# A two-layer graph-attention and feed-forward kernel: engines in a written order of phases, expert rows in pairs of tiles added to the output by accumulating scatters, and a dense last batch

## Chip, cores and metric

The kernel runs on one core of one Trainium2 chip. The metric is device time in microseconds of one execution; smaller is better. The time of the kernel before is 2003.29 us, the median of three runs (2002.27 to 2005.84).

## What is computed

The input x has 64 batches of 256 nodes with 256 features, all float32. One 256 x 256 adjacency matrix serves all batches. Two layers follow each other, and every step adds to x:

```python
x = x + elu(gat4(layernorm(x), adj))        # layer 0: graph attention, 4 heads of 64
x = x + layernorm(x) @ Wf.T + bf            # layer 0: one linear map
x = x + relu(gat1(layernorm(x), adj))       # layer 1: graph attention, 1 head of 256
x = x + moe(layernorm(x))                   # layer 1: mixture of experts
# moe(t): top 2 of 8 experts by router logits, weights rw normalized to a sum of 1
#   out = t + sum over the two experts e of rw_e * (gelu(t @ w1[e] + b1[e]) @ w2[e] + b2[e])
```

The mixture adds its own input, so the last line leaves x + t + the two weighted expert results for each of the 16384 tokens.

## The kernel before

A batch is 256 tokens, two tiles of 128 (NT = 2). `batch_layers` (L353 to L435) is a Python generator that records one batch: layer norm statistics on VectorE (L273, L274) and GpSimd (L276, L277), transposes on TensorE (L284) that ScalarE copies out of PSUM (L288), projections (L298) whose logits ScalarE exponentiates (L306) and VectorE scales (L310), attention weights z (L325 transposes, L332 on VectorE), their product with the values (L343), the linear map (L386, L392), the second attention, and the last layer norm xng (L416). From it come the router logits (L431, L435), and x + xng, formed by GpSimd (L423), is stored in a scratch array `base` (L424).

Experts are computed on routed rows only. Batches are taken in chunks of four (eight tiles), chunks in three groups of 28, 24 and 12 batches (`GROUPS`). `dispatch` (L447 to L569) runs once per chunk, on VectorE almost alone: top two experts, a count of the rows of each expert, the place of each row in a region of the expert, and a list of slots that are full by now. GpSimd then sends every token's row twice, to the regions of its two experts, by indirect DMAs of 128 rows (`send`, L573). `slot` (L604 to L673) handles one tile of 128 rows of one expert: SyncE loads the expert's weights `we` (L613) and the rows `xr` (L617), with expert and place in registers; TensorE transposes the rows (L631, copied by ScalarE at L633), multiplies by w1 (L644), ScalarE applies gelu (L650), TensorE multiplies by w2 (L656), VectorE adds the bias (L663), and GpSimd scatters the 128 results (L668) to a scratch array `y`, where each token has one row for each of its two experts. When all slots of a group are done, `combine` (L675 to L695) loads for each tile of tokens its two rows of `y` (L681) and its row of `base` (L679), adds them with the routing weights in two VectorE instructions (L692) and stores the result (L695). Partly filled tiles are topped up with filling rows at the end of each group, which makes 277 slots in all (2 x 128 + 3 x 7).

Order of the work: the main loop at the end starts a batch every three steps (`TICKS`), hands out slots and merges at a rate (`Rate`), and calls every active generator once per step. That is only the order in which instructions are recorded; the framework's scheduler then orders each engine's instructions by priority and readiness as its own model sees them. Each engine runs its list strictly in order. PSUM holds eight such buffers of one bank, divided by tag: two for `tr` (all transposes, attention logits, counts), three for `mm` (projections, attention results, linear map, router logits), three for `sl` (expert products). Loads and stores are all issued from SyncE's one queue, indirect DMAs from GpSimd's.

```python
        if step % TICKS == 0 and more:
            nxt = next(batches, None)
...
        for job in slots.start():
            active.append(job())
        for job in merges.start():
            active.append(job())
        for job in list(active):
            if next(job, active) is active:
                active.remove(job)
```

Of the kernel before, what the change touches and what calls it, by code (L numbers as in the profile page):

```python
# [8 lines left out]
F32 = mybir.dt.float32  # L9
# [5 lines left out]
P = 128  # L15
SLOT_ENGINES = [mybir.EngineType.SP, mybir.EngineType.PE, mybir.EngineType.DVE]
AFTER = mybir.DependencyInfo(mybir.DependencyClass.Sync, mybir.DependencyReason.DATA)
# [8 lines left out]
def kernel(  # L26
# [20 lines left out]
    H = 4  # L47
# [9 lines left out]
    GROUPS = ((4,) * 7, (4,) * 6, (4, 4, 2, 2))  # L57
    assert sum(map(sum, GROUPS)) == B
    NTC = max(map(max, GROUPS)) * NT
    SLOTS = 2 * NTC + 2 * (E - 1)  # L60

    ROW = D + 2
    YPAD = 2 * 2 * E * P
# [7 lines left out]
    psum = ctx.enter_context(tc.tile_pool(name="psum", bufs=2, space=bass.MemoryType.PSUM))  # L71

# [27 lines left out]
    for layer, op in enumerate((ALU.is_gt, ALU.not_equal)):  # L100
        mf = work.tile([P, NT, N], F32, tag="xT", name=f"maskf{layer}", bufs=4)
        nc.vector.tensor_scalar(mf, adj_i, 0.0, None, op0=op)
        pm = psum.tile([P, NT, N], F32, tag="tr", name="pm")
        for t in range(NT):
            for j in range(NT):
                nc.tensor.transpose(
                    pm[:, j, t * P : (t + 1) * P], mf[:, t, j * P : (j + 1) * P], ident
                )
        m = const.tile([P, NT, N], F32, tag=f"mask{layer}", name=f"mask{layer}")
        nc.vector.tensor_copy(m, pm)  # L110
        masks.append(m)

    def center(w, cols):


        pc = psum.tile([P, cols], F32, tag="mm", name="pc", bufs=3)
# [47 lines left out]
    pw = psum.tile([P, KT, D], F32, tag="tr", name="pw")  # L164
# [15 lines left out]
    pr = psum.tile([P, KT, E], F32, tag="tr", name="pr")  # L180
# [7 lines left out]
    WBUFS = 6  # L188
# [3 lines left out]
    def pack_expert(e):  # L192
# [8 lines left out]
        )  # L201
        nc.sync.dma_start(
# [3 lines left out]
        nc.sync.dma_start(out=b2s[:, e, :], in_=rows_to_all(b2[e], D))  # L206
        nc.sync.dma_start(out=wpack[e], in_=wt)

    caps = [sum(g) * NT + 1 for g in GROUPS]
    xs_d = [
        tc.dram_tile([(E * cap + E) * P, ROW], F32, name=f"xs_{g}")
        for g, cap in enumerate(caps)
    ]
    y_d = [
        tc.dram_tile([YPAD + 2 * sum(n) * N, D], F32, name=f"y_{g}") for g, n in enumerate(GROUPS)
    ]
    base_d = [tc.dram_tile([sum(n) * N, D], F32, name=f"base_{g}") for g, n in enumerate(GROUPS)]


    fill = const.tile([P, E, ROW], F32, tag="fill", name="fill")
    nc.gpsimd.memset(fill, 0.0)
    nc.vector.memset(fill[:, :, D : D + 1], -1.0)
    nc.gpsimd.iota(
        fill[:, :, D + 1 : D + 2], pattern=[[2 * P, E], [1, 1]], base=0, channel_multiplier=2,
        allow_small_or_imprecise_dtypes=True,
    )

    def fill_spare():  # L230
        for xs, cap in zip(xs_d, caps):
            nc.sync.dma_start(
                out=xs[E * cap * P :, :].rearrange("(t p) c -> p t c", p=P), in_=fill
            )
        nc.vector.tensor_scalar(
            fill[:, :, D + 1 : D + 2], fill[:, :, D + 1 : D + 2], 2.0 * E * P, None, op0=ALU.add
        )

# [9 lines left out]
    )  # L248
    def iota(shape, pattern, base, by_partition, name):
# [6 lines left out]

    em8 = iota([E], [[1, E]], -E, 0, "em8")
    jrow = iota([SLOTS], [[1, SLOTS]], 0, 0, "jrow")
    tok2 = iota([NTC], [[2 * P, NTC]], 0, 2, "tok2")
    part = iota([1], [[1, 1]], 0, 1, "part")  # L260
    region = []
    for g, cap in enumerate(caps):
        region.append(iota([E], [[cap, E]], 0, 0, f"region{g}"))
    scan_mask = const.tile([P, E, NTC], F32, tag="scan_mask", name="scan_mask")
    nc.vector.memset(scan_mask, 1.0)
    nc.vector.memset(scan_mask[:, :, 0:1], 0.0)

# [12 lines left out]
    def transposed(src):  # L280
        pt = psum.tile([P, KT, N], F32, tag="tr", name="pt")
# [9 lines left out]
    def projected(xT, wx, heads, rstd):  # L291
# [3 lines left out]
        for t in range(NT):  # L295
            pq = psum.tile([P, heads, d + 3], F32, tag="mm", name="pq", bufs=3)
# [19 lines left out]
    def attention(q, heads, mask):  # L316

        d = D // heads
        probs = []
        for h0 in range(0, heads, 2):  # L320
            hs = range(h0, min(h0 + 2, heads))
            pd = psum.tile([P, len(hs), N], F32, tag="tr", name="pd")
            for i, h in enumerate(hs):
                for t in range(NT):
                    nc.tensor.transpose(  # L325
                        pd[:, i, t * P : (t + 1) * P],
                        q[:, t, h, d + 1 : d + 2].to_broadcast([P, P]), ident,
                    )
            for i, h in enumerate(hs):
                z = work.tile([P, NT, N], F32, tag="z", name="z", bufs=6)  # L330
                for j in range(NT):
                    nc.vector.scalar_tensor_tensor(  # L332
                        z[:, j, :], pd[:, i, :], q[:, j, h, d + 2 : d + 3], mask[:, j, :],
                        op0=ALU.max, op1=ALU.mult,
                    )
                probs.append(z)
            yield
        pvs = []
        for t in range(NT):
            pv = psum.tile([P, heads, d + 1], F32, tag="mm", name="pv", bufs=3)  # L340
# [12 lines left out]
    def batch_layers(b, g, r0, c0, xng, lg):  # L353
# [6 lines left out]
        yield  # L360
        q = projected(xT, wx0, H, rstd)
        yield
        pvs, rinv = yield from attention(q, H, masks[0])
        hp = work.tile([P, NT, D], F32, tag="hp", name="hp")
        for t, pv in enumerate(pvs):
# [3 lines left out]
            )  # L369
        ex = work.tile([P, NT, D], F32, tag="e", name="e")  # L370
        nc.scalar.activation(ex, hp, AF.Exp)  # L371
        yield
# [4 lines left out]
        _, rstd = norm_stats(x1)  # L377
        yield
        xT = transposed(x1)
        x1b = work.tile([P, NT, D], F32, tag="x1b", name="x1b")  # L380
        nc.gpsimd.tensor_add(x1b, x1, bias_f[:, None, :].to_broadcast([P, NT, D]))
        yield
        pf = psum.tile([P, NT, D], F32, tag="mm", name="pf", bufs=3)
# [12 lines left out]
        yield  # L396
        _, rstd = norm_stats(x2)
        yield
        xT = transposed(x2)
        yield  # L400
        q = projected(xT, wx1, 1, rstd)
        yield
        pvs, rinv = yield from attention(q, 1, masks[1])
# [6 lines left out]
        yield  # L410
        mv, rstd = norm_stats(x2)
        yield
        xe = keep.tile([P, NT, ROW], F32, tag="xng", name="xng", bufs=XNG)
        xn = xe[:, :, :D]
        for t in range(NT):
            nc.vector.tensor_scalar(  # L416
                xn[:, t, :], x2[:, t, :], mv[:, t, 0:1], rstd[:, t : t + 1],
                op0=ALU.subtract, op1=ALU.mult,
            )
        xng.append(xe)  # L420
        yield
        xT = transposed(xn)
        nc.gpsimd.tensor_add(x2, x2, xn)  # L423
        nc.sync.dma_start(  # L424
            out=base_d[g][r0 * P : (r0 + NT) * P, :].rearrange("(t p) d -> p t d", p=P), in_=x2
        )
        yield
        pl = psum.tile([P, NT, E], F32, tag="mm", name="pl", bufs=3)
# [6 lines left out]
        nc.vector.tensor_copy(lg[:, c0 : c0 + NT, :], pl)  # L435

    XNG = max(map(max, GROUPS)) + 3

    def whole(out, in_, name):
# [5 lines left out]
    def dispatch(g, c, nt, done, n, first, last, xng, lg, state):  # L445


        rt = lambda shape, name, bufs=1, dt=F32: keep.tile(
            [P] + shape, dt, tag=name, name=f"{name}_{g}_{c}", bufs=bufs
        )  # L450
        vec, tt = nc.vector, nc.vector.tensor_tensor
        emb = em8[:, None, :].to_broadcast([P, nt, E])
        ohs, tops, lcur = [], [], lg
        for k in range(2):
# [10 lines left out]
            if k == 0:  # L465
                for i, xe in enumerate(xng):
                    vec.tensor_scalar(
                        xe[:, :, D : D + 1], least[:, i * NT : (i + 1) * NT, None], float(E), None,
                        op0=ALU.add,
                    )  # L470
                    vec.tensor_scalar(
                        xe[:, :, D + 1 : D + 2], tok2[:, i * NT : (i + 1) * NT, None],
                        float(YPAD + 2 * P * done), None, op0=ALU.add,
                    )
# [4 lines left out]
            tops.append(top)  # L479
        m = rt([E, nt], "m")  # L480
        tt(m.rearrange("p e t -> p t e"), ohs[0], ohs[1], ALU.add)
        mf = m.rearrange("p e t -> p (e t)")

        pp = psum.tile([P, 2, E, nt], F32, tag="tr", name="pp")
# [5 lines left out]
        yield  # L490
        ed = rt([nt], "ed")
        tt(ed, tops[1], tops[0], ALU.subtract)
        nc.scalar.activation(ed, ed, AF.Exp)
        run = rt([E, nt], "run")
        if nt == NTC:
            vec.tensor_tensor_scan(
                run.rearrange("p e t -> p (e t)"), scan_mask.rearrange("p e t -> p (e t)"),
                both[:, 1].rearrange("p e t -> p (e t)"), 0.0, ALU.mult, ALU.add,
# [8 lines left out]
        rows, used = state  # L507
        at = rt([E], "at")
        vec.scalar_tensor_tensor(at, region[g], float(P), rows, op0=ALU.mult, op1=ALU.add)
        tt(pre, pre, at[:, :, None].to_broadcast([P, E, nt]), ALU.add)  # L510
        tt(rows[:, :, None], rows[:, :, None], run[:, :, nt - 1 : nt], ALU.add)
        wts = rt([2, nt], f"wts_{g}_{c}")
        vec.tensor_scalar(wts[:, 0], ed, 1.0, None, op0=ALU.add)
        vec.reciprocal(wts[:, 0], wts[:, 0])
        tt(wts[:, 1], ed, wts[:, 0], ALU.mult)
# [5 lines left out]
        vec.tensor_copy(pos, posf)  # L521
        if last:
            tt(at, at, run[:, :, nt - 1], ALU.add)
            pads = rt([E], "pads", 1, I32)
            tt(pads, at, part.to_broadcast([P, E]), ALU.add)
        else:
            pads = None
        yield

        full = rt([E], "full")  # L530
        vec.tensor_scalar(
            full, rows, 1.0 / P, (127.0 / P if last else 0.0) - 127.0 / 256.0,
            op0=ALU.mult, op1=ALU.add,
# [306 lines left out]
```

## Time and profile before

| What | Value |
|---|---|
| median of 3 runs | 2003.29 us |
| the profiled execution: its time, its span | 1986.96 us, 1985.2 us |
| mean granted TensorE clock | 0.911 |
| TensorE busy, x10244 | 1609.9 us (81%) |
| VectorE busy, x4618 | 1284.2 us (65%) |
| GpSimd busy, x1278 | 1063.7 us (54%) |
| ScalarE busy, x1770 | 819.5 us (41%) |
| ScalarE activation-table loads (L650 109, L306 102, L493 5, two more) | 218 at 1283 ns |
| DMA queue q1 (SyncE's): bytes, share of 16 engines | 230.32 MB, 38.2% |
| DMA queue q0 (GpSimd's): bytes, share of 16 engines | 73.33 MB, 10.0% |

How to read it: "busy" is the time in which an engine had an instruction in it, over the span, which runs from the first instruction to the last. The granted clock is the share of TensorE's full speed that its throttle let through, so a TensorE that is busy at a granted clock of 0.9 does nine tenths of the work. A matrix product of float32 is recorded as two instructions, a transpose as one. No engine is busy all the time, so the views that matter are those by stretch of time and those of waits.

### The profile page before, as it was taken

How to read it: one execution, taken by the hardware profiler on the slowest of the kernel's cores; microseconds unless marked ns; L12 is line 12 of the kernel's file. 1: busy time of each engine (PE TensorE's matmuls, PEld its weight loads, DVE VectorE, ACT ScalarE, POOL GpSimd, SP SyncE). 2: the span in 40 equal slices, each digit the busy share in tenths (PEclk: the TensorE clock that was granted, in tenths of full speed). 3: DMA queues.
4: the chain of work that ended last, by engine and by line, in shares of the span. 5: the costliest groups of instructions: out<-in, count | busy, mean ns of one | idle time of the engine just before them, and what ended most of it. 6: DMA issues, size and time to landing. Idle time of an engine off the chain costs nothing. (4 is left out here: it accounts for less than half of the span.)

```text
span 1985.2 us, 34359 instructions
## 1 busy us (share of the span) xinstructions
PE 1609.9 (81%) x10244; PEld 1431.6 (72%) x10244; DVE 1284.2 (65%) x4618; ACT 819.5 (41%) x1770; POOL 1063.7 (54%) x1278
## 2 busy tenths in 40 slices
PE   6988979799979897787988979897989879677800
PEld 5877878688868786776877868786878768676700
DVE  7886857476757675664566968786756645552444
ACT  1222344354545455344544535463535434342400
POOL 2455555556465647555555655656575554664400
PEclk9998889898989999898998989998989989898955
DMA  8113223434333434244445566666543434587987
GB/s 270 61 44 108 68 73 116 134 118 141 113 126 124 145 112 143 92 134 127 146 130 174 175 193 207 222 192 191 178 149 112 130 118 137 167 259 244 314 263 235
DMA packets 211096, 306.84 MB, mean 155 GB/s; under 512 B 29880, under 2 KB 140096, under 8 KB 210912
## 3 DMA queue, kind: packets, MB, share of 16 engines
q1 hardware_dynamic: 183184, 230.32, 38.2%
q0 software_dynamic: 26736, 73.33, 10.0%
q8 instruction: 84, 1.38, 0.3%
q10 hardware_dynamic: 992, 0.99, 0.2%
q14 instruction: 100, 0.82, 0.1%
HBM read 192.16 MB, written 112.38 MB: 153 GB/s over the span
## 5 line engine op out<-in xcount | busy, mean ns | idle before, releaser
L343 PE MATMUL pv<-q,z 128*128 128x65 f32 (+1 forms) x2560 | 386.4, 307 | 46.7 <-DVE q L310 33.5
L668 POOL DMA_INDIRECT y<-y,to x277 | 292.4, 1056 | 243.4 <-DVE mv L274 83.3
L343 PEld LDWEIGHTS pv<-q,z 128*128 128x128 f32 x2560 | 347.0, 202 | 69.5 <-DVE q L310 42.5
L644 PE MATMUL ph<-sT,we 128*128 128x128 f32 x2216 | 297.9, 285 | 38.2 <-DVE y L663 18.9
L644 PEld LDWEIGHTS ph<-sT,we 128*128 128x128 f32 x2216 | 288.8, 201 | 49.7 <-DVE y L663 20.0
L573 POOL DMA_INDIRECT xs<-xng,pos x256 | 253.3, 989 | 91.5 <-issue 68.1
L656 PE MATMUL py<-w2s,hT 128*128 x1108 | 298.4, 401 | 2.9 <-ACT hT L650 2.9
L332 DVE SCALAR_TENSOR_TENSOR z<-pd,q,mask 128x256 f32<-128x256 f32 x640 | 268.3, 473 | 33.8 <-PE pd L325 33.4
L298 PE MATMUL pq<-wx,xT 128*128 128x268 f32 (+1 forms) x1024 | 270.6, 399 | 2.3 <-ACT xT L288 2.2
L650 ACT ACTIVATE hT<-ph,we 128x128 f32<-128x128 f32 x554 | 170.0, 365 | 190.9 <-PE ph L644 140.7
L276 POOL TENSOR_SCALAR rstd<-mv 128x2 f32<-128x2 f32 x256 | 64.1, 251 | 297.2 <-DVE mv L274 271.0
L656 PEld LDWEIGHTS py<-w2s,hT 128*128 128x128 f32 x1108 | 204.6, 201 | 24.8 <-ACT hT L650 4.0
L288 ACT COPY xT<-pt 128x512 f32<-128x512 f32 x256 | 146.3, 588 | 148.4 <-PE pt L284 147.7
L298 PEld LDWEIGHTS pq<-wx,xT 128*128 128x128 f32 x1024 | 184.2, 195 | 26.1 <-ACT xT L288 2.7
L273 DVE BATCH_NORM_STATS2 stats<-x 128x6 f32<-128x256 f32 x384 | 148.9, 410 | 81.5 <-POOL x L409 79.7
L636 DVE SCALAR_TENSOR_TENSOR to<-xr,ef 128x1 int32<-128x1 f32 x277 | 76.4, 279 | 187.7 <-DMA xr<-xs 126.8
L277 POOL TENSOR_TENSOR rstd<-rstd,mhalf 128x2 f32<-128x2 f32 x256 | 186.7, 729 | 19.9
L371 ACT ACTIVATE e<-hp 128x512 f32<-128x512 f32 x64 | 40.3, 629 | 336.9 <-DVE hp L366 336.8
L650 ACT ACT_TABLE_LOAD x109 | 139.8, 1283 | 72.3 <-issue 41.7
L692 DVE SCALAR_TENSOR_TENSOR o<-yk,wts,o 128x256 f32<-128x256 f32 x256 | 123.1, 499 | 71.2 <-DMA o<-base 48.4
L310 DVE SCALAR_TENSOR_TENSOR q<-pq,rstd,q 128x256 f32<-128x256 f32 x256 | 116.0, 476 | 59.5 <-ACT q L306 59.1
L306 ACT ACT_TABLE_LOAD x102 | 130.9, 1283 | 49.6 <-PE pq L298 48.7
(135 smaller groups left out, 2338.3 us busy)
## 6 DMA issues: line engine op xcount, KB each, us to landing
we<-wpack SPq DMA_DIRECT2D x277, 288.0 KB
xr<-xs SPq DMA_DIRECT2D x277, 129.0 KB
yk<-y SPq DMA_DIRECT2D x128, 256.0 KB
xin<-in_x_dram SPq DMA_DIRECT2D x64, 256.0 KB
base<-x SPq DMA_DIRECT2D x64, 256.0 KB
o<-base SPq DMA_DIRECT2D x128, 128.0 KB
out_dram<-o SPq DMA_DIRECT2D x128, 128.0 KB
y<-y,to POOLq DMA_INDIRECT x277, 3.5
```

Of the source, the lines that this page charges most:

```text
L273: nc.vector.bn_stats(stats[:, t, :], src[:, t, :])
L277: nc.gpsimd.tensor_tensor(rstd, rstd, mhalf, ALU.pow)
L288: nc.scalar.copy(dst, pt)
L298: nc.tensor.matmul(pq.rearrange("p h c -> p (h c)"), xT[:, k, t * P : (t + 1) * P], wx[:, k, :], start=(k == 0), stop=(k == KT - 1),)
L306: nc.scalar.activation(q[:, t, :, d:], pq[:, :, d:], AF.Exp, scale=rstd[:, t : t + 1])
L332: nc.vector.scalar_tensor_tensor(z[:, j, :], pd[:, i, :], q[:, j, h, d + 2 : d + 3], mask[:, j, :], op0=ALU.max, op1=ALU.mult,)
L343: nc.tensor.matmul(pv[:, h, :], z[:, j, t * P : (t + 1) * P], q[:, j, h, : d + 1], start=(j == 0), stop=(j == NT - 1),)
L573: d = nc.gpsimd.indirect_dma_start(out=xs_d[g][: E * caps[g] * P, :], out_offset=bass.IndirectOffsetOnAxis(ap=at, axis=0), in_=xe, in_offs ...
L644: nc.tensor.matmul(ph[:, f, :], we[:, k * D + f * P : k * D + (f + 1) * P], xT[:, k, :], start=(k == 0), stop=(k == KT - 1),)
L650: nc.scalar.activation(hT[:, f, :], ph[:, f, :], AF.Gelu, bias=we[:, C_B1 + f : C_B1 + f + 1])
L656: mm = nc.tensor.matmul(py, hT[:, f, :], w2s[:, bass.ds(e, 1), f * D : (f + 1) * D].rearrange("p e c -> p (e c)"), start=(f == 0), stop=(f ...
L668: d = nc.gpsimd.indirect_dma_start(out=y_d[g][:, :], out_offset=bass.IndirectOffsetOnAxis(ap=to, axis=0), in_=y, in_offset=None,)
```

## The change

The same results are computed with the following differences (lines are those of the changed kernel):

- **Written order.** The main loop runs inside a manual schedule: each engine executes its instructions in the order in which they are recorded. Each generator yields a rank, and within a step the active generators are called in the order of their ranks. Phases are merged and split a little, and the routing (`route`, formerly `dispatch`) is spread over four steps instead of being recorded in two.
- **PSUM.** All tiles share one pool of eight buffers.
- **Pairs.** An expert's rows are handled in pairs of tiles (256 rows): one load of weights, one of rows, one bias addition of 512 elements, products with 256 moving columns. There is one group over 63 batches with one region for each expert (`CHUNKS` of 4 batches, then 2 and 1), which makes 126 + 7 = 133 pairs. The first chunk has only one pair that is surely full, each later one eight; 14 pairs are left to a flush at the end, where filling rows are written by SyncE.
- **Rows carry more.** Each sent row has its token number, first expert and two weights in four extra columns (260 instead of 258 elements).
- **No `y`, no `base`, no `combine`.** ScalarE forms xng and x + xng by two activations with per-row scale and bias instead of VectorE and GpSimd, and x + xng is stored straight to the output. ScalarE multiplies an expert's results by their weights (L644), and GpSimd adds them to the output's rows by two indirect DMAs per pair that accumulate (L682). A pair's two scatters wait for the two scatters of the pair before it, and for the stores of x + xng recorded since.
- **Dense last batch.** Batch 63 is not routed: after its router, all eight experts are applied to its 256 rows with the weights (zero for six of them) folded in by VectorE (L711), and its result is stored once, after the last scatter.

Instructions of the program, before and after: TensorE's expert products with w1 are 1108 of 128 columns, then 564 of 256; with w2 554, then 564 of 256; table loads 218, then 106; loads of `we` and `xr` 277 each, then 133 each; scatters of results 277, then 266; sends 256 and 24 of filling rows, then 252. The written order has 251 steps: a batch starts at every third step up to 189, the first result of a pair is scattered at step 47, the last layers of batch 63 are at step 206, and 30 of the 133 pairs are scattered after step 208.

The diff, cut to its core:

```diff
-    GROUPS = ((4,) * 7, (4,) * 6, (4, 4, 2, 2))
+    CHUNKS = (4,) * 15 + (2, 1)
...
+    def bank(name, shape):
+        t = psum.tile([P, 2 * D], F32, tag="bank", name=name, bufs=8)
...
-        for t in range(NT):
-            nc.vector.tensor_scalar(
-                xn[:, t, :], x2[:, t, :], mv[:, t, 0:1], rstd[:, t : t + 1],
-                op0=ALU.subtract, op1=ALU.mult,
...
-        nc.gpsimd.tensor_add(x2, x2, xn)
+        for t in range(NT):
+            nc.scalar.activation(
+                xe[:, t, :D], x2[:, t, :], AF.Identity, bias=by[:, 0, t : t + 1],
+                scale=rstd[:, t : t + 1],
+            )
+        for t in range(NT):
+            nc.scalar.activation(
+                base[:, t, :], x2[:, t, :], AF.Identity, bias=by[:, 0, t : t + 1],
+                scale=by[:, 1, t : t + 1],
+            )
...
+    def expert_pair(j, n, ids, ef, regs, needs):
...
+        yield 30
+        hT = hidden(xT, we)
+        yield 80
...
+        y = result(hT, bass.ds(regs["x"][i], 1))
+        yield 2
+        for t in range(2):
+            nc.scalar.activation(y[:, t, :], y[:, t, :], AF.Copy, scale=w[:, t : t + 1])
+        scatters.append((y, to))
...
+    def scatter():
...
+        y, to = scatters.pop(0)
+        ds = []
+        for t in range(2):
+            ds.append(nc.gpsimd.indirect_dma_start(
+                out=out_rows, out_offset=bass.IndirectOffsetOnAxis(ap=to[:, t : t + 1], axis=0),
+                in_=y[:, t, :], in_offset=None, compute_op=ALU.add,
+            ))
...
+            before = added[-2:] + based
...
+            for ins in before:
+                tc.add_manual_dep(ds[-1].ins, ins.name, AFTER, reason="added to before")
...
+    with tc.manual_schedule():
+        while more or active or waiting or scatters:
+            phase = step % TICKS
+            if phase == 0 and more:
...
+            if phase == 2:
+                credit = min(credit + (2.0 if more else 3.0), 3.0)
+                while waiting and credit >= 1.0:
+                    credit -= 1.0
+                    begin(waiting.pop(0)(), 90)
+            if scatters:
...
+                begin(one(), 55 if phase == 1 else 5)
+            for entry in sorted(active, key=lambda a: a[:2]):
+                entry[0] = next(entry[2], None)
```

## The prediction

> **What bounds the kernel now.** I read the page's busy shares first, then the slices, then stretches, and last TensorE's waits. (Columns of a stretch: length, busy time of TensorE, its weight loads, VectorE, ScalarE and GpSimd with counts, granted clock, DMA share, GB/s.)
>
> ```profile
> PE 1609.9 (81%) x10244; PEld 1431.6 (72%) x10244; DVE 1284.2 (65%) x4618; ACT 819.5 (41%) x1770; POOL 1063.7 (54%) x1278
> ...
> PEclk9998889898989999898998989998989989898955
> ```
>
> ```profile
> 700.00:730.00 30.00, 29.52 (x200) 26.33 (x198) 20.79 (x64) 17.60 (x37) 15.59 (x20) 1.00 0.43 132
> 1600.00:1700.00 100.00, 91.05 (x612) 82.28 (x611) 56.10 (x218) 48.05 (x110) 46.79 (x54) 0.99 0.41 128
> 300.00:1300.00 1000.00, 869.91 (x5627) 776.97 (x5628) 674.86 (x2435) 473.42 (x990) 583.53 (x694) 0.94 0.45 144
> 0.00:200.00 200.00, 165.70 (x1013) 142.21 (x1014) 151.85 (x555) 46.70 (x109) 91.06 (x139) 0.95 0.39 120
> ```
>
> ```profile
> 1700.00:1880.00 180.00, 138.31 (x831) 122.92 (x830) 77.73 (x311) 63.97 (x180) 97.63 (x104) 0.90 0.79 255
> 1880.00:1985.00 105.00, 4.52 (x30) 3.84 (x28) 47.44 (x105) 2.00 (x6) 4.48 (x5) 0.54 0.81 250
> ```
>
> TensorE carries the kernel up to 1880 us; after that come 105 us of `combine` alone (loads of `y`, two VectorE additions, stores). Busy time times clock is work at full speed: 1610 x 0.911 = 1467 us. So 518 of the 1985 us are gaps, slow clock and tail. In the steady middle the yield is 0.87 x 0.94 = 0.82; the best 100 us reach 0.91 x 0.99 = 0.90. What are the gaps? TensorE's waits say:
>
> ```profile
> PE pt L284 <- DVE z L332: 87.4, 32, 21.7
> PE pv L343 <- DVE q L310: 33.5, 17, 7.2
> PE pf L386 <- DVE lg L435: 23.6, 5, 8.4
> PE ph L644 <- DVE y L663: 18.9, 5, 9.7
> ```
>
> (total, times, longest.) A transpose cannot read z, so it waits for a PSUM buffer that VectorE has yet to drain; the longest, 21.7 us, fit routing, whose rows (L442 to L568) sum to 226 us, 13 us per chunk. No engine is full: the order binds.
>
> **TensorE's work does not change.** Full-speed prices come from 712 to 728 us, start to start:
>
> ```profile
> 714.22 3.68 PE L343 MATMUL pv<-q,z 128*128 128x65 f32 x32
> 717.74 1.08 PE L656 MATMUL py<-w2s,hT 128*128 x4
> 718.66 1.95 PE L644 MATMUL ph<-sT,we 128*128 128x128 f32 x16
> 720.44 0.38 PE L631 MATMUL px<-ident,xr 128*128 128x128 f32 x2
> 720.66 1.97 PE L298 MATMUL pq<-wx,xT 128*128 128x268 f32 x8
> ```
>
> So a batch's pv of 65 columns costs 3.52, pq 1.81 and again 1.84, its 257-column pv 1.82, pf 1.72, pl 0.81, and 26 transposes 2.82: 14.3 us. A slot costs 0.22 + 0.89 + 0.86 = 1.97. Before: 64 x 14.3 + 277 x 1.97 = 1464, which agrees with 1467. After: products of 256 columns cost 0.215 a record (py), so a pair costs 0.44 + 1.72 + 1.72 = 3.9, and a dense expert 3.44: 64 x 14.3 + 133 x 3.9 + 8 x 3.44 = 1461. Pairing halves weight loads on TensorE, which already lie beside the products. Nothing is gained here.
>
> **The other engines.** VectorE: out go `combine` (L692, 123 us), xng (50), the `to` rows (76) and 17 net on y (277 x 0.415 against 141 x 0.69, the price of the 512-element L375/L376); in come 399 two-element operations at 0.2 (80), `by` 22, dense 8; about 1130. ScalarE: 112 table loads fewer x 1.283 = -144; gelu and sT -60 by larger tiles; scaling of results 266 x 0.42 = +112 and xng with base 256 x 0.42 = +107 (0.42 lies between L650's 0.365 for 128 elements and L406's 0.476 for 256): about 835. GpSimd: L423 -77, filling sends -24, 15 other DMAs -15: about 950. All stay well under TensorE's, so these edits count as nothing in the sum; the cover is TensorE's yield, and if that reached 0.95, VectorE (18 us of a 23 us batch) would be next. DMA: `we` falls from 277 x 288 KB to 133, `yk` and the reload of base vanish; q1 goes from 230 to some 120 MB. Its waits (xr, 127 us on VectorE) show only where they hold TensorE.
>
> **SyncE's queue** loses its worst blocker (L424 waited 513 us for GpSimd's addition); now it waits for ScalarE's base one step later, with xr and we behind it, each two steps ahead of use. That slack, some 15 us, hides it.
>
> **The new wait.** Each pair's scatters wait for the previous pair's. Behind them in GpSimd's queue stand rstd, x1b, rel and the sends, and so ScalarE's exponentials. An ordinary scatter:
>
> ```profile
> L668 POOL DMA_INDIRECT y<-y,to x277: 957/1067/1321, 219.5 to 1885.7; - x139
> ...
> DMA to landing us min/median/max: 2.4/3.5/5.8
> ```
>
> One pair takes the second issue's delay (0.96 + 0.30 = 1.27), the landing, and 0.30 to go on. No row shows an accumulating DMA. Lower end: the fastest landing, 2.4, so 4.0 us per pair. Upper end: reading first and then writing, twice the slowest, 11.6, so 13.2. Below nothing is excluded: it moves the same rows. I take the nearest row's median, 3.5: 5.1 us. In the middle, two pairs come in about 24 us, mostly in different steps, so it costs nothing there; at the end 30 pairs stand in a row.
>
> The Trainium skill speaks against this edit: "DMA: Bandwidth & Descriptors", Rules for kernel authors, says an accumulate reads its destination and writes later, so that others' writes in between are lost and one must wait for the earlier semaphore; the change obeys it and pays with this chain. The same page, Anatomy of one DMA, puts a software-generated DMA at 2.0 us plus bytes / 436e3, 2.3 us for 128 KB; the trace's 3.5 is longer, and by the page's figure the 28 pairs of the tail below would cost 34 us less.
>
> **The sum**, by stretches of the written order, with TensorE's full-speed work in each (counted from its phases):
>
> - steps 0 to 42, layers only, 177 us of work. At the yield of the first 200 us (0.83 x 0.95 = 0.79): 225; +15 because 18 steps fill an empty pipeline: **240**.
> - steps 43 to 189, 1060 us. In the written order TensorE's inputs come a step (7 us) earlier, except pq after pt, which waits about 0.4 us for ScalarE; routing is spread over four steps, and eight shared buffers, of 23 that a batch with its pairs uses, cover a lag of a third of a period. But GpSimd's step with rel (1.29), a pair's scatters (2.54), x1b (1.29), two rstd (0.98 each) and two sends (2.54) sums to 9.6 us against TensorE's 6.6 (pd, pq, two pt, two py). Yield between 0.82 and 0.90, I take 0.87: **1218**. The ends give 1293 and 1178.
> - steps 190 to 208, 89 us at 0.8 because two chunks route at once: **111**.
> - steps 209 on, 136 us of work, but the chain is longer: 12 us until the first results (a load 3, then px, copy, ph, table, gelu, py, addition, scaling), 8 pairs x 5.1 = 41, dense experts 28 less about 15 that four waiting y cover, 8 to begin again, 20 x 5.1 = 102, one store 4: **180**.
>
> Sum 1749, and with 1.8 us around the span 1751, against the profiled 1987 (-236). That execution lies 0.8% below the median of the runs; scaled by 2003.29 / 1986.96, **1765 us**.
>
> **Rivals.**
>
> - *The written order stalls.* For it: VectorE must follow in order now, and its waits for TensorE and ScalarE inside a phase (rinv for pv 112 us, q for ScalarE 59 us in total) can no longer be filled by other work. Against: those waits stand off TensorE's path today. At a yield of 0.76: 1395 + 250 + 115 + 190 = 1950 in the span, **1965**; still faster. At 0.72 it is slower than before.
> - *The accumulating chain binds throughout*, which ends slower. Place: L682 in GpSimd's queue. It decides from the point where 133 pairs after the first scatter (265 us) fill the rest: (1985 - 265) / 133 = 12.9 us per pair, a landing of 11.3. For it: an unmeasured kind of DMA, and upper bound 13.2. At a landing of 14: 265 + 133 x 15.6 + 20 = **2360**. Against: it takes three times the median of the plain scatter.
> - *The order brings nothing* (the change does not do what it says): yield stays 0.82 and only the tail changes: 240 + 1293 + 111 + 180, scaled **1840**.
>
> **How the numbers follow.** My forecast 1765 with the 1840 case as its slow side (1680 to 1850): 0.58. Stalls, still faster (1850 to 1999): 0.19. Better than 1680 (yield over 0.92, landing 2.4): 0.04. Within 0.2%, about what this measurement can tell: 0.02. Slower: the chain 0.07, deep stalls 0.10. So faster 0.81, same 0.02, slower 0.17. Range: 1680 from 0.90 and 4.0 us per pair (-40, -31, -15 at the start); 1960 from stalls, or the chain's upper bound in the tail (+227).
>
> **What would show it.** Right: TensorE busy over 90% from 300 to 1400 us at a clock of 0.96; no waits over 10 us for z; 106 table loads; about 180 us after batch 63's layers, with GpSimd's DMAs some 5 us per pair apart and ScalarE's and VectorE's y waiting for them. Wrong: TensorE waiting for a VectorE that idles; landings over 8 us; GpSimd's rstd waiting for DMA in the middle.

## The result, and the profile after

The changed kernel takes **2212.43 us** (median of 4 runs, 2206.59 to 2215.49) where the kernel before takes 2004.57 beside it: a ratio of 1.1035 [1.1009, 1.1061]. The forecast was 1765, faster. The profiled execution took 2215.49 us.

From its page, the busy shares and the granted clock by slices:

```profile
PE 1669.7 (75%) x9154; PEld 1463.0 (66%) x9154; DVE 1228.5 (55%) x4443; ACT 836.9 (38%) x1765; POOL 1092.8 (49%) x1172
...
PEclk9999989898887979888897989888897978589775
```

The same steady stretch as before, by the view of stretches (length, busy time of TensorE, weight loads, VectorE, ScalarE, GpSimd, then granted clock, DMA share, GB/s):

```profile
300.00:1300.00 1000.00, 805.17 (x4468) 711.35 (x4467) 600.74 (x2129) 419.96 (x872) 533.70 (x573) 0.87 0.36 89
```

TensorE's yield there is 0.805 x 0.87 = 0.70, against 0.82 before and 0.87 as forecast. TensorE's waits, the longest ones:

```profile
PE pd L342 <- DVE q L330: 174.0, 22, 12.6
PE ph L651 <- ACT sT L623: 88.2, 11, 15.9
PE pv L363 <- DVE y L672: 83.1, 11, 7.8
PE px L619 <- DMA xr<-xs: 49.4, 4, 40.9
```

The waits for z are gone. pd (the transposes for the attention weights, L342) waits for q instead (the exponentiated logits, which ScalarE makes at L326 and VectorE scales at L330), and q can be followed back in the view of all engines' waits:

```profile
POOL out_dram L682 <- DMA out_dram<-y,to: 375.8, 123, 5.9
...
DVE q L330 <- ACT q L326: 342.7, 88, 16.2
...
ACT q L326 <- POOL rstd L297: 313.4, 46, 15.5
```

TensorE waits for VectorE, that for ScalarE, that for GpSimd's rstd; and GpSimd itself stands 376 us at L682, the scatter, for an earlier scatter to land, 243 us of it before the last layers end. Its timeline (start, duration, line) shows one such passage; x1b is x with the linear map's bias added:

```profile
745.35 1.62 POOL L682 DMA_INDIRECT out_dram<-y,to  x1 [0.17 <-issue]
749.45 1.56 POOL L682 DMA_INDIRECT out_dram<-y,to  x1 [2.49 <-DMA out_dram<-y,to]
750.48 1.83 POOL L404 TENSOR_TENSOR x1b<-x,bias_f 128x512 f32<-128x512 f32 x1
751.71 0.81 POOL L296 TENSOR_SCALAR rstd<-mv 128x2 f32<-128x2 f32 x1
```

The two scatters at 745 and 749 are of one pair, and the second waits for the first; x1b and rstd stand behind. The tail shows the price without other work:

```profile
2159.91 1.55 POOL L682 DMA_INDIRECT out_dram<-y,to  x1 [3.03 <-DMA out_dram<-y,to]
2164.45 1.55 POOL L682 DMA_INDIRECT out_dram<-y,to  x1 [2.98 <-DMA out_dram<-y,to]
```

Every scatter, not every pair, comes 4.55 us after the last: 9.1 us per pair. The code says why: `declare_no_dep` for the group "out" frees a scatter only from instructions that are in the group by then, and both scatters of a pair join it after the loop (run e1 below tests this). So the description above, by which a pair waits only for the pair before it, does not hold of what ran.

Below, a run is cut at two marks: the first px (transposes of a pair's rows) and the last pl (router logits). **Middle** is from the one to the other, **end** from there to the end of the span. For the changed kernel they come from the views of the tiles px and pl ("first and last start"):

```profile
L619 PE MATMUL px<-ident,xr x532: 272/273/475, 239.2 to 2132.8; 128*128 128x128 f32 x178
```

```profile
L477 PE MATMUL pl<-rT,xT x512: 171/256/362, 92.4 to 1869.2; 128*128 128x8 f32 x171
```

Middle 1869 - 239 = 1630, end 2213.5 - 1869 = 344. The forecast had 240 to the first px, then 1218 + 111 = 1329, then 180: the start is right, the middle lost 301 and the end 164. The second mark lies some two steps ahead of the step 209 at which the sum's last stretch begins, so the split between the two is rough.

### The profile page after: what moved, and what is told of

Read it like the earlier page. It is cut to its first block, busy times and chain, and to the rows that moved or that the text cites. A ratio compares the mean times of both kernels' runs of the same rounds, so it can differ in the third digit from the quotient of the medians.

```text
span 2213.5 us, 29807 instructions
## 1 busy us (share of the span) xinstructions
PE 1669.7 (75%) x9154; PEld 1463.0 (66%) x9154; DVE 1228.5 (55%) x4443; ACT 836.9 (38%) x1765; POOL 1092.8 (49%) x1172
## 3 DMA queue, kind: packets, MB, share of 16 engines
q0 software_dynamic: 50400, 68.44, 18.5%
## 5 line engine op out<-in xcount | busy, mean ns | idle before, releaser
L682 POOL DMA_INDIRECT out_dram<-y,to x266 | 420.8, 1582 | 598.0 <-DMA out_dram<-y,to 375.8
L651 PE MATMUL ph<-sT,we 128*128 128x256 f32 x1064 | 298.5, 444 | 94.1 <-ACT sT L623 88.2
L651 PEld LDWEIGHTS ph<-sT,we 128*128 128x128 f32 x1064 | 239.9, 231 | 137.1 <-ACT sT L623 90.5
L330 DVE SCALAR_TENSOR_TENSOR q<-pq,rstd,q 128x256 f32<-128x256 f32 x256 | 112.1, 479 | 354.1 <-ACT q L326 342.7
L666 PE MATMUL py<-w2s,hT 128*128 (+1 forms) x1128 | 257.8, 383 | 0.0
L342 PE MATMUL pd<-ident,q 128*128 128x128 f32 x640 | 117.4, 305 | 178.4 <-DVE q L330 174.0
L644 ACT ACTIVATE y<-y,w 128x256 f32<-128x256 f32 x266 | 116.4, 498 | 352.6 <-DVE y L672 332.6
L672 DVE TENSOR_TENSOR y<-py,b2s 128x512 f32<-128x512 f32 x141 | 94.7, 689 | 262.2 <-DMA out_dram<-y,to 145.9
L342 PEld LDWEIGHTS pd<-ident,q 128*128 128x128 f32 x640 | 87.1, 154 | 197.7 <-DVE q L330 179.9
L326 ACT ACTIVATE q<-pq,rstd 128x12 f32<-128x12 f32 (+1 forms) x256 | 55.4, 264 | 322.2 <-POOL rstd L297 313.4
L657 ACT ACTIVATE hT<-ph,we 128x256 f32<-128x256 f32 x266 | 109.9, 471 | 134.2 <-PE ph L651 69.2
```

The source lines that it names most:

```text
L342: nc.tensor.transpose(pd[:, i, t * P : (t + 1) * P], q[:, t, h, d + 1 : d + 2].to_broadcast([P, P]), ident,)
L644: nc.scalar.activation(y[:, t, :], y[:, t, :], AF.Copy, scale=w[:, t : t + 1])
L651: nc.tensor.matmul(ph[:, f, :], we[:, k * D + f * P : k * D + (f + 1) * P], xT[:, k, :], start=(k == 0), stop=(k == KT - 1),)
L666: nc.tensor.matmul(py[:, t, :], hT[:, f, t * P : (t + 1) * P], w2s[:, e, f * D : (f + 1) * D].rearrange("p e c -> p (e c)"), start=(f == 0 ...
L682: ds.append(nc.gpsimd.indirect_dma_start(out=out_rows, out_offset=bass.IndirectOffsetOnAxis(ap=to[:, t : t + 1], axis=0), in_=y[:, t, :], ...
```

## The experiments

Beside these runs the kernel before took 1995 to 2017 us, so times compare across runs to about 1%; ratios are against the kernel before, and a run without a ratio was executed once. In the expectations C means that the chain of waiting scatters holds GpSimd's queue, W that the written order itself stalls, A that accumulating costs more than a plain scatter; B and Q, that a waiting scatter costs by what stands behind it in the queue; T, that the chain's throughput or traffic costs wherever it stands.

| Run | us | middle | end | us per pair at the end |
|---|---|---|---|---|
| changed kernel | 2212 | 1630 | 344 | 9.1 |
| e1_pair_together | 1924 | 1425 | 262 | 6.3 |
| e2_plain_scatter | 1953 | 1442 | 270 | 6.3 |
| e14_plain_together | 1797 | 1334 | 214 | 4.5 |
| e4_no_scatter | 1747 | 1333 | 172 | none |

### The chain's price

**e1**: the second scatter of a pair no longer waits for the first.

```diff
             for ins in before:
                 tc.add_manual_dep(ds[-1].ins, ins.name, AFTER, reason="added to before")
+            tc.add_to_no_dep_group("out", ds[-1].ins)
         based.clear()
         for d in ds:
-            tc.add_to_no_dep_group("out", d.ins)
             added.append(d.ins)
```

> Edit: the first scatter of a pair joins the group of permitted neighbours before the second is declared, so the second no longer waits for the first; both still wait for the pair before. Theory C (chain: the changed kernel's time goes into the accumulating scatters' chain, which blocks GpSimd's queue and so rstd and ScalarE's exponentials): a pair's price falls from 2 x 4.55 = 9.1 us to about 6.2 (1.57 + 0.3 + a landing of some 4.3); the last 30 pairs save 85 us and the middle, where GpSimd is blocked 3 us less per pair, another 100 to 150: about 1990 us. Theory W (the written order itself stalls, scatters or not): only the end gains, about 2125 us.

1923.78 us, ratio 0.9623 [0.9572, 0.9675]: moving this one line turns the change from a loss into a gain. The tail (the last wait is put down to ScalarE's hT here, but the distance of 6.3 us is that of the pairs beside it):

```profile
1862.54 1.55 POOL L682 DMA_INDIRECT out_dram<-y,to  x1 [3.08 <-DMA out_dram<-y,to]
1864.40 1.55 POOL L682 DMA_INDIRECT out_dram<-y,to  x1 [0.31 <-issue]
1868.88 1.55 POOL L682 DMA_INDIRECT out_dram<-y,to  x1 [2.93 <-ACT hT L657]
```

**e2**: `compute_op=ALU.add` removed, serial waits kept; results replace rows instead of being added. **e14**: the same in e1.

> Edit: the scatters overwrite instead of accumulating (left out: the addition; the output then holds the last writer's row), all waits kept. Theory A (accumulation itself is the cost: 1.57 us of issue against 1.06 for a plain one, and a slower landing): a link falls from 4.55 to about 3.4 us, the end saves 60 x 1.1 = 66 us and the middle most of its 300 us excess: about 1900 us. Theory C: the chain of 266 links stays and is only a quarter shorter: about 2080 us.

> Edit: pairs go together, and the scatters overwrite instead of accumulating (left out: the addition). It prices accumulation alone against the kernel whose pairs go together (middle 1425, end 262). A pair's price falls from 6.34 to about 0.95 + 0.30 + 0.95 + 2.2 = 4.4 us: end about 215, and the middle, whose step with rstd is held up by 2.2 instead of 3.4 us, about 1385: about 1840 us. If accumulation costs nothing but its issue time, only the middle changes, about 1890.

1952.76 (3.15 us from scatter to scatter) and 1797.04 us. The tail of e14:

```profile
1737.88 0.96 POOL L682 DMA_INDIRECT out_dram<-y,to  x1 [4.52 <-DMA out_dram<-y,to]
1739.14 0.96 POOL L682 DMA_INDIRECT out_dram<-y,to  x1 [0.30 <-issue]
1742.38 0.96 POOL L682 DMA_INDIRECT out_dram<-y,to  x1 [2.27 <-DMA out_dram<-y,to]
```

**e4**: no scatters at all; expert results are computed and dropped.

> Edit: no scatters at all (left out: adding the experts' results to the output); everything else in the same written order. Theory C: the middle returns to a yield near 0.87 (25 us per batch instead of 31) and the end to TensorE's 136 us plus loads: about 1800 us. Theory W: the middle stays near 31 us per batch, only the end gains 150 us: about 2050 us.

1746.69 us. The marks of its middle:

```profile
L619 PE MATMUL px<-ident,xr x532: 272/273/477, 240.7 to 1730.5; 128*128 128x128 f32 x178
```

```profile
L477 PE MATMUL pl<-rT,xT x512: 170/256/257, 94.4 to 1573.3; 128*128 128x8 f32 x171
```

e1 and e4 speak for C and against W. e2 does not: 1953 lies nearer A's 1900 than C's 2080, so accumulating is part of the cost beside the double wait. e1 and e2 pay the same 6.3 us per pair in different ways, one by accumulating, one by waiting twice, and lose nearly the same in the middle (92 and 109 us over e4's 1333). At 4.5 us the middle loses 1 us, at 9.1 it loses 297.

The prices of the tail are not what the middle pays. From 300 to 1300 us the view of lines gives for L682:

| Run | scatters | busy us | idle before, us | sum per pair, us | loss of the middle, us |
|---|---|---|---|---|---|
| changed kernel | 122 | 194.0 | 231.6 | 7.0 | 297 |
| e1 | 142 | 225.8 | 70.6 | 4.2 | 92 |
| e2 | 141 | 137.4 | 181.7 | 4.5 | 109 |
| e14 | 150 | 146.5 | 41.5 | 2.5 | 1 |

In e1 only 12.6 of the 70.6 us are put down to an earlier scatter; most of what holds the queue there is the issue of the scatters themselves. So in these four the middle follows how long a pair holds GpSimd's queue, by its issue as well as by its wait.

### The written order

**e5**: the changed kernel without `tc.manual_schedule()`. **e11**: e1 without it; its scatters keep the places that they have in e1.

> Edit: the manual schedule is taken away, the framework's scheduler orders each engine's instructions by its own model; pairs, scatters, chain and shared PSUM buffers stay. Theory W: the scheduler fills the stalls, 28 us per batch as in the kernel before, so about 2080 us. Theory C: the scheduler's model does not know the chain's price, so GpSimd is blocked as before or worse: 2150 to 2300 us, and the last pairs still go out 9.1 us apart.

> Edit: pairs go together, and the manual schedule is taken away (the framework's scheduler orders each engine). It tells what the written order is worth once the chain is mended. Theory W' (the written order is worth little): about 1925 us. Theory C: the scheduler, which does not know the chain, leaves rstd behind waiting scatters: 2246 less 85 at the end and less 80 in the middle, about 2080 us.

2245.61 and 2050.77 us. W falls: without the written order the kernel is not faster. Once the pair is mended, the written order is worth 2051 - 1924 = 127 us.

### What stands behind a waiting scatter

**e7**: the serial second scatter is recorded later in its step, behind x1b and rstd. **e8**: the same in e1. **e9**: e1 with eight y buffers instead of four.

```diff
-                begin(one(), 55 if phase == 1 else 5)
+                begin(half(0), 55 if phase == 1 else 5)
+                begin(half(1), 97 if phase == 1 else 58)
```

> Edit: the changed kernel with its serial scatters, but the second scatter of a pair stands further back in GpSimd's written order: behind x1b and the two rstd in the step that has them (rank 58 instead of right behind the first; 97 where the first has 55). The chain of 266 links of 4.55 us is untouched. Theory B (what costs in the middle is that rstd and x1b stand behind a waiting scatter in GpSimd's queue): 1630 us from the first pair to the last layers fall to about 1430, as where the wait is gone; the end stays 344: about 2010 us. Theory T (the chain's throughput or its traffic costs, wherever it stands): 2190 to 2215 us.

> Edit: both mends, a pair's two scatters not waiting for each other, and the second one behind x1b and rstd. Theory B: rstd is then held up by one issue (1.9 us) instead of two (3.4): the middle falls from 1425 to about 1380, the end stays near 262: about 1885 us. Theory T: no change against the kernel whose pairs go together, 1924 us.

> Edit: pairs go together, and eight buffers of y instead of four. If the end (262 us) waits for buffers that the chain holds, TensorE runs ahead there and the chain starts its 30 pairs earlier: 20 to 40 us less, about 1895 us; the middle, where VectorE waited only 12 us for a free y, stays. If the chain alone bounds the end (30 x 6.3 = 190 us from its first result on): no change, 1924 us.

2100.67, 1940.49 and 1916.24 us (ratios of the last two 0.9734 [0.968, 0.9788] and 0.9619 [0.9564, 0.9675]). In e7, 114 us of the middle came back (1517), none of the end: partly what was expected. e8 missed: it is no faster than e1, rather slower, and why is not shown. e9's ratio is nearly that of e1.

**e12**: e9 with scatters at rank 97 in phase 1 and none in phase 0 while layers run. **e13**: e12 with the dense experts after the flush, in two result buffers of their own.

```diff
-            if scatters:
+            if scatters and (phase or "xT" in last_batch):
...
-                begin(one(), 55 if phase == 1 else 5)
+                begin(one(), 97 if phase == 1 else 5)
```

> Edit: pairs go together, eight buffers of y, and while layers run no scatter is put into the step that holds x1b and the two rstd; one pair goes first in the step after next, one last in the step between. Theory B: nothing urgent stands behind a scatter any more, the middle falls from 1418 to about 1360, the end stays 255: about 1860 us. If GpSimd's load itself is what is left (it has two pairs' issues, 7.4 us, in a batch of 24), the middle stays and so does the time, 1916 us.

> Edit: as the run before, and the eight dense experts come after the flush pairs instead of in front of them, with two y buffers of their own, so that TensorE's 28 us of them lie beside the chain. If the chain of the last 30 pairs (30 x 6.3 us) bounds the end: 15 to 30 us less than the run before, about 1835 us. If the end is bound by its beginning (loads that wait for the last sends): no change.

2037.55 and 2031.51 us (1.0206 [1.0162, 1.025] and 1.0179 [1.0128, 1.023]). e12 is a clear miss, its middle grew to 1523; e13 does not differ from it beyond the noise, so where the dense experts stand is worth nothing clear. GpSimd's timeline of e12:

```profile
829.72 1.61 POOL L682 DMA_INDIRECT out_dram<-y,to  x1 [0.30 <-issue]
831.64 1.59 POOL L682 DMA_INDIRECT out_dram<-y,to  x1 [0.31 <-issue]
839.40 1.56 POOL L682 DMA_INDIRECT out_dram<-y,to  x1 [6.17 <-DMA out_dram<-y,to]
841.27 1.55 POOL L682 DMA_INDIRECT out_dram<-y,to  x1 [0.30 <-issue]
843.12 0.99 POOL L742 DMA_INDIRECT xs<-xng,pos  x1 [0.30 <-issue]
```

Rank 97 in one step and rank 5 in the next put two pairs in a row, so the second wait (6.17 us) is paid in full, ahead of sends, x1b and rstd. What seems to count is a distance between pairs and nothing urgent behind them; the edit mended the one by spoiling the other. The cause needed a sharper test: take the batches' work off GpSimd's queue piece by piece.

**e15**: the changed kernel, but users of rstd read a constant; GpSimd still computes rstd, so the normalizing scale is left out. **e18**: e15 with both additions on VectorE and eight y buffers. **e19**: e18 with the pairs' rows loaded from the input instead of from the sent rows, destinations always rows 0 to 255. **e17**: e18's edits in e1.

```diff
-        return mv, rstd
+        return mv, ones[:, :NT]
...
-        nc.gpsimd.tensor_add(x1b, x1, bias_f[:, None, :].to_broadcast([P, NT, D]))
+        nc.vector.tensor_add(x1b, x1, bias_f[:, None, :].to_broadcast([P, NT, D]))
...
-        nc.gpsimd.tensor_add(x2, x2, rel)
+        nc.vector.tensor_add(x2, x2, rel)
```

> Edit: the changed kernel with its serial scatters in their places; GpSimd still computes every rstd, but nobody reads it: all consumers take a constant one (left out: the layer norms' scale; by and xng change with it). Theory B (the middle is lost because ScalarE's exponentials and VectorE's x2 wait for rstd behind waiting scatters): the middle falls from 1630 to 1430 us or less, the end stays 344, about 2010 us. Rival (x1b and rel, which stand in the same queue, or the chain's traffic do it): at least 1580 in the middle, 2160 us or more.

> The changed kernel with its serial scatters, but no compute of the batches hangs on GpSimd's queue any more: the two adds (x1b and x+rel) are done by VectorE, eight y buffers instead of four, and the consumers of rstd use a constant (GpSimd still computes rstd). What is left out: the scaling by rstd. Only the sends and the scatters on GpSimd still matter. Theory Q (a waiting scatter costs by what stands behind it in GpSimd's queue: rstd, x1b, x+rel, and the y buffers that it holds): the stretch from the first px to the last pl falls from 1630 us to 1400 or less, the end stays near 344, about 1970 us in all. Rival T (the accumulating traffic itself, or the loads behind the sends, slow the middle): the stretch stays at 1500 or more, 2080 us or more.

> As the serial kernel without batch compute on GpSimd's queue (2061 us), and the pairs' rows are loaded from the input instead of from the sent rows, so that the loads wait for no send; destinations are the rows 0 to 255 each time. What is left out: the routing of rows, besides the scaling by rstd. Sends and scatters are still issued, in their order. Theory Q (what is left of the middle's loss stands behind the scatters too, through the sends that the loads of xr wait for): the stretch from the first px to the last pl falls from 1460 us to 1330 to 1370; TensorE's wait for xr, 138 us, is gone. Rival T (the accumulating traffic): it stays above 1430. The end stays the chain's, 340 us or more, so 1930 to 1980 us by Q, over 2020 by T.

> As the kernel with two scatters of a pair issued together and eight y buffers (1916 us), with the two adds on VectorE and the consumers of rstd using a constant; the scaling by rstd is left out. Q: the stretch from the first px to the last pl falls from 1418 to about 1345, near the 1333 of the kernel without scatters, about 1845 us in all. T: it stays above 1400, 1900 us or more.

| Run, serial scatters | us | middle | | Run, pair together | us | middle |
|---|---|---|---|---|---|---|
| changed kernel | 2212 | 1630 | | e9 | 1916 | 1418 |
| e15, rstd not awaited | 2137 | 1546 | | e16, additions moved | 1899 | 1385 |
| e18, and additions moved, 8 y | 2061 | 1460 | | e17, and rstd not awaited | 1833 | 1328 |
| e19, and sends not awaited | 1935 | 1325 | | | | |

e15 and e18 missed what each expected, and each time the wait moved to the next thing in the queue. TensorE's first wait in e18, 49 us in the changed kernel:

```profile
PE px L619 <- DMA xr<-xs: 137.6, 15, 53.2
```

With that gone too, e19's middle is 1325, at or below the 1333 without scatters, while its 266 accumulating scatters still wait serially (GpSimd stands 270 us for them, 132 of it from 240 to 1570 us) and its end is 365. So the whole loss of the middle went through GpSimd's queue: in this order of removal 84 us by rstd, 86 by the additions and the y buffers, 135 by the sends. e17 says the same with the pair together and the rows sent and scattered as routed (middle 1328), so the accumulating traffic takes nothing from the middle by itself. The steady stretch of e19:

```profile
300.00:1300.00 1000.00, 938.68 (x5480) 838.72 (x5479) 743.91 (x2693) 516.50 (x1074) 557.71 (x619) 0.95 0.43 106
```

### A version that keeps the whole computation

**e16**: e9 with the two additions on VectorE. **e20**: e16 with each step's scatters placed behind that step's rstd, still one pair in each step.

```diff
-                begin(one(), 55 if phase == 1 else 5)
+                begin(one(), 75 if phase == 1 else 45)
```

> A version that computes all: scatters of a pair together, eight y buffers, and the adds x1b and x+rel on VectorE (0.69 us for 128x512 there against 1.27 to 1.85 on GpSimd). Q: rstd no longer stands behind x1b and x2 no longer behind a scatter, a third of the 84 us that the middle still loses comes back: about 1885 us. T: no gain, 1910 to 1920.

> The version with the adds on VectorE (1899 us), its scatters placed in each step behind that step's rstd instead of ahead of it, still one pair in each step, so evenly spaced (the placement that failed bunched them in two adjacent steps). Q: nothing of the batches stands behind a waiting scatter within its step; the stretch from the first px to the last pl falls from 1385 us to about 1350, about 1865 us in all. Rival: the wait reaches over the step's end as in the placements tried so far, no gain or a loss, 1900 to 1930.

e16 takes 1898.67 us, ratio 0.9416 [0.938, 0.9452]. e20 takes **1842.08 us**, 0.9232 [0.9202, 0.9262], the fastest kernel with the whole computation, below its expected 1865; its middle is 1338:

```profile
L619 PE MATMUL px<-ident,xr x532: 272/273/476, 243.8 to 1762.7; 128*128 128x128 f32 x178
```

```profile
L477 PE MATMUL pl<-rT,xT x512: 171/256/256, 94.1 to 1582.0; 128*128 128x8 f32 x171
```

GpSimd's timeline:

```profile
723.76 0.75 POOL L297 TENSOR_TENSOR rstd<-rstd,mhalf 128x2 f32<-128x2 f32 x1
724.51 0.25 POOL L296 TENSOR_SCALAR rstd<-mv 128x2 f32<-128x2 f32 x1
724.85 0.71 POOL L297 TENSOR_TENSOR rstd<-rstd,mhalf 128x2 f32<-128x2 f32 x1
725.73 1.63 POOL L682 DMA_INDIRECT out_dram<-y,to  x1 [0.18 <-issue]
727.66 1.55 POOL L682 DMA_INDIRECT out_dram<-y,to  x1 [0.30 <-issue]
738.09 0.22 POOL L296 TENSOR_SCALAR rstd<-mv 128x2 f32<-128x2 f32 x1 [8.88 <-DVE mv L294]
```

In this passage the pair goes out when no norm is due, 11.6 us after the pair before it, and GpSimd then waits for VectorE rather than for a DMA. Its waits for scatters are 51 us in all, after 376 in the changed kernel, 71 in e1 and 110 in e16. From 300 to 1300 us a pair holds the queue for 4.2 us, as in e1 (148 scatters, 237.3 us busy, 69.9 idle before), but the middle loses 5 us instead of 92. So what counts is what stands behind the pair, and not only how long it holds the queue. The end, 257 us, is still the chain's.

## Why the prediction was wrong

The failed step is **the new wait**, in both of its halves.

- *The price*, "5.1 us per pair". It was 9.1. The sum assumed that only the first scatter of a pair waits, as the code seems to say; the second waits too, which doubles the landing. And accumulating is dearer at both ends: issue 1.57 instead of 0.96 us, landing 3.9 at the median where 3.5 was taken (the plain scatters of e14 landed in 2.4). Of 9.1 - 4.5 = 4.6 us, mending the wait saves 2.8 (e1), plain scatters alone also 2.8 (e2); the two overlap. The upper bound, 13.2, held it, but only as a tail cost.
- *"It costs nothing there"*, in the middle. True at 4.5 us in the places of the change (e14 loses 1 us), false there at 6.3 and 9.1. The step named rstd, x1b, rel and the sends as standing behind, then compared a pair's price only with the distance between pairs. But by its own count the 9.6 us of a busy GpSimd step already exceeded TensorE's 6.6, so a wait or an issue ahead of rstd had no slack. That loss is 301 of the 464 us by which the profiled span, 2213.5, exceeds the sum, 1749.
- *The end*, "30 pairs stand in a row": right in kind. 28 x 9.1 in place of 28 x 5.1 gives 112 of the 164 us that were missing. Another 46 are five more pairs: GpSimd's timeline has 33 pairs behind the last pl, where the sum priced 28, and 33 x 9.1 is 300 of the 344 us.

What held: TensorE's work (1669.7 x 0.856 = 1429 in this trace, 1599.9 x 0.921 = 1474 in e20's, 1461 forecast); the first px at 239 us for 240; the middle without scatters, 1333 in e4 for 1329 (the marks are not quite the sum's steps, so that a difference as small as 4 us is in part luck); q1's 121 MB for 120. ScalarE's sum is right too, 837 for 835. VectorE's is 98 us short and GpSimd's 143 (of which the issues of the scatters are 266 x (1.582 - 1.067) = 137); the first seems to have cost nothing, as VectorE has 1202 us in e4 too, where the middle is as forecast. The slow end of the range does not follow from its own term: 1765 + 227 is 1992, not 1960, and the measured time lies beyond both.

Of the rivals, the *stalling order* fell: e4's middle is within 4 us of the forecast with the order kept, and without the order e5 is no faster. *The order brings nothing* fell by the same middle. *The accumulating chain* had the right place, L682 in GpSimd's queue, but the wrong mechanism and point: it was to decide from 12.9 us per pair, where the chain alone fills the time. It decided far below, through what queues behind it. The last of the signs of being wrong, rstd waiting for DMA in the middle, is what the trace shows, if a wait ahead of rstd in its queue is counted.

## What to carry to other kernels

A wait on an in-order queue, and the issue of the waiting instruction with it, costs by what stands behind it and by that work's slack, long before the chain itself fills the time: list what is behind, and place the waiting instruction after whatever is due in the step, with distance between two such. When one thing behind it is taken away, the next in the queue shows the wait, so test by removing all of it as well as one. Read from a trace, not from the code, which instruction waits for which: a freeing declaration holds only for what is registered when it is made.

## What the runs showed of the hardware

An accumulating scatter of 128 rows of 1 KB costs more at each end than a plain one. The views of the output's scatters, e1 (accumulating) and then e14 (plain; durations in ns, then landing in us):

```profile
L682 POOL DMA_INDIRECT out_dram<-y,to x266: 1537/1577/1680, 274.9 to 1921.9; - x133
...
DMA to landing us min/median/max: 3.6/3.9/8.0
```

```profile
L682 POOL DMA_INDIRECT out_dram<-y,to x266: 957/963/1177, 278.9 to 1785.8; - x133
...
DMA to landing us min/median/max: 2.4/2.4/4.8
```

The Trainium skill's "DMA: Bandwidth & Descriptors", Anatomy of one DMA, puts a software-generated DMA at 2.0 us plus bytes / 436e3, which makes an estimate of 2.3 us for 128 KB. The plain landings of e14 agree with it at 2.4; the accumulating ones do not, and neither does the median of the kernel before, 3.5 for its plain scatters. The accumulating scatters also moved the same bytes in more packets, GpSimd's queue in e1 and in e14 (packets, MB, share of 16 engines):

```profile
q0 software_dynamic: 50400, 68.44, 20.4%
```

```profile
q0 software_dynamic: 24864, 68.44, 10.5%
```

That is (50400 - 24864) / 266 = 96 packets more for each scatter. TensorE's granted clock from 300 to 1300 us was 0.87 at 81% busy in the changed kernel and 0.95 at 94% in e19, so that there an idle TensorE was also a slower one. But at 89% it was 0.89 in e18 and 0.94 in e1: the busy share alone does not set it, and what does was not tested.
